# Two bank counts and a filling order in the attention stream of a fused two-layer kernel

## The chip, the cores and the metric

The kernel runs on one core of a Trainium2 chip. The time is the device time of one execution in microseconds: 1094.37 us is the median of three runs of the kernel before (1093.66 to 1094.58). The engines are named as in the profile: PE is the matrix engine (PEld its weight loads), DVE the vector engine, ACT the scalar engine, POOL the general engine, SP the engine that issues most transfers.

## The reference, cut to what matters

The input is x of 2 batches x 512 positions x 512 channels. Four blocks are added to it in turn, each on its layer norm:

```python
x = x + attn_a(_layernorm(x))   # 32 heads of 128, 8 key/value heads, weights as 4-bit codes and scales
x = x + ffn(_layernorm(x))      # 8 low-rank experts (rank 64), the two best of each position, softmax gate
x = x + attn_b(_layernorm(x))   # 32 heads of 16, 8 key/value heads, weights in f32
x = x + ffn(_layernorm(x))      # the same experts again
```

Attention b, which the change is about, is

```python
att = einsum('bhgqd,bhkd->bhgqk', q, k) / sqrt(16)       # q, k turned by the position
att = where(causal, att, -inf)
probs = softmax(att)
out = einsum('bhgqk,bhkd->bhgqd', probs, v) -> (B, T, 512) @ Wo
```

Everything is f32 at the interface.

## The kernel before, in words

The first 60% of the time or so is attention a, and it is not touched by the change. The rest is a sequence with three parts: the first experts ("f1") of both batches with the projections of attention b of batch 0; then the stream, in which the scores of attention b of both batches run while other work fills PE; then an end, with the last output projection and the second experts ("f2") of batch 1.

**The stream.** Attention b has 32 pairs of key heads and query groups (2 batches, 2 halves of the key heads, 4 groups, 2 pairs); each pair takes 3 steps, and all of it 96 steps and 8 more. Two generators are advanced once a step. `maxima` (from L765) multiplies queries with keys into two score banks `sc_b` (L781), and DVE takes each row's maximum out of them (L785); POOL splits the maximum into two parts `mm` (L793, L794); four steps after a pair began, `maxima_in` turns `mm` with PE (`tpm`, L804) and ACT casts it into two rows beside the queries (L807). Eight steps after a pair's maxima, `probabilities` multiplies keys with these longer queries into two banks `st_b` (L828): the scores come transposed and with the maximum taken off. ACT takes the exponential into `pT_b` (L834) and POOL clears what lies above the diagonal (L837). One step's scores are one of three groups: a whole row of 512 columns for two heads, 384 columns, or 128 and 256 together.

Every sixth step `weighted_b` multiplies the probabilities of a group with the values (`num_b`, L854): 32 matmul instructions, in four column strips side by side, into one bank of their own. ACT copies the sums out (L865), and transfers carry the denominators to memory and back for `divided`, which yields the quotients `oN_b` that `output_b` projects (`po`, L910) and adds to x (L914).

**The filling work.** `side` is a chain of generators: the rest of the experts f1 of batch 1 (`py_f`, L266), the projections of batch 1 (normed and turned x `pxT_b`, L178; keys and values `pkv_b`, L674; turned keys `tpk`, L666; queries `pq_b`, L701; turned queries `tpq`, L694), the output projection of batch 0 in two parts, the experts f2 of batch 0 (`pxT_f`, `pg_f` L197, `ph_f` L207, `lg_f` L217, `wT_f` L259, `py_f`), and the first part of the output projection of batch 1. Each `yield` gives the cost of a piece: `MM` = 0.9, about two instructions of 512 columns (one f32 product of 128 rows is two instructions). In each step, after the scores and the value products, pieces are drawn until their costs have used up the `pace` of the step: 0.8 until step 8, 0.95 until step 44, 0.37 until step 66, 0.95 again, 1.4 from step 90.

**Order.** In the stream, `tc.manual_schedule(engines={mybir.EngineType.PE})` keeps PE's instructions in the order of the program; PE runs them in that order, and an instruction that waits holds up all that follow. The other engines' order is planned by the compiler.

**Banks.** PSUM has eight banks. From the end of attention a on they are three pools: `ps_x` with 5 banks for `sc_b`, `st_b` and `tpm` in turn, `ps_n` with 1 for the value products, and `ps_f` with 2 for the filling pieces of the stream (`place("bank", ...)` with `banks = BESIDE`). Outside the stream the experts and projections take their banks from `ps_x` (`ALONE`). A tile of a pool takes the place of the tile that many allocations earlier, and its first matmul waits until the last reader of that one is done. A filling tile is read by `rope_heads` on DVE (L639, L641; for keys also by two copies of the values on ACT, L681), by copies on ACT (L179, L199, L211, L695), by a cast on ACT and a difference on DVE (`halves`, L151, L152), or by a DVE addition or product (L261, L270, L914).

Of the kernel before, what the change touches and what calls it, by code (L numbers as in the profile page):

```python
# [17 lines left out]
PSUM = bass.MemoryType.PSUM  # L18
# [22 lines left out]
def kernel(  # L41
# [113 lines left out]


    MM = 0.9
    def norm_parts(b, which):

        var = small.tile([P, NT, 2], F32, tag="mv", name=f"mv_{which}_{b}")  # L160
        for t in range(NT):
            st = small.tile([P, 6], F32, tag="st", name=f"st_{which}_{b}_{t}")
            nc.vector.bn_stats(st, x[b, t])
            nc.vector.bn_aggr(var[:, t, :], st)
        std = small.tile([P, NT], F32, tag="std", name=f"std_{which}_{b}")
        nc.scalar.activation(std, var[:, :, 1], AF.Sqrt, bias=eps)
        rstd = small.tile([P, NT], F32, tag="rstd", name=f"rstd_{which}_{b}")
        nc.vector.reciprocal(rstd, std)
        yield 3.0
        xT = place("xT", [P, NC, S], f"xnT_{which}_{b}")  # L170
        for t in range(NT):
            xn = place("xn", [P, DM], f"xn_{which}_{b}_{t}")
            nc.vector.tensor_scalar(
                xn, x[b, t], var[:, t, 0:1], rstd[:, t : t + 1], ALU.subtract, ALU.mult
            )
            pt = place("bank", [P, NC, P], f"pxT_{which}_{b}_{t}")
            for c in range(NC):
                nc.tensor.transpose(pt[:, c, :], xn[:, ts(c, P)], ident)  # L178
            nc.scalar.copy(xT[:, :, ts(t, P)], pt)  # L179
            yield MM  # L180
        return xT

    def experts(b, which, store):

        xT = yield from norm_parts(b, which)
        nm = f"{which}_{b}"

        def st(tag, n=1):
            return gate.tile([P, NT, n], F32, tag=tag, name=f"{tag}_{nm}")

        def each(a):
            return a.to_broadcast([P, NT, NE])


        pg = place("bank", [P, S], f"pg_{nm}")
        for c in range(NC):
            nc.tensor.matmul(pg[ts(c, STRIP)], gw[:, c, :], xT[:, c, :], start=True, stop=True)  # L197
        shares = place("xn", [P, S], f"shares_{nm}")
        nc.scalar.copy(shares, pg)  # L199
        yield MM  # L200
        hT = place("hT", [P, NC, S], f"hT_{nm}")

        def ranks(er):

            ph = place("bank", [P, S], f"ph_{nm}_{er}")
            for c in range(NC):
                nc.tensor.matmul(  # L207
                    ph, lora["a"][:, c, ts(er, P)], xT[:, c, :], start=(c == 0), stop=(c == NC - 1)
                )
                if c == NC - 1:  # L210
                    nc.scalar.copy(hT[:, er, :], ph)  # L211
                yield MM

        yield from ranks(0)
        lg = place("bank", [P, NT, NE], f"lg_{nm}")
        for t in range(NT):
            nc.tensor.matmul(lg[:, t, :], shares[:, ts(t, P)], fold, start=True, stop=True)  # L217
        mx, pr, den, rden = st("gmx"), st("gp", NE), st("gden"), st("grden")
        nc.vector.tensor_reduce(mx, lg, AX.X, ALU.max)
        nc.vector.tensor_tensor(pr, lg, each(mx), ALU.subtract)  # L220
        nc.scalar.activation(pr, pr, AF.Exp)
        nc.vector.tensor_reduce(den, pr, AX.X, ALU.add)
        nc.vector.reciprocal(rden, den)
        nc.vector.tensor_tensor(pr, pr, each(rden), ALU.mult)
        yield MM


        best, hot = [], []
        left = pr
        for n in range(2):  # L230
            m, key, km, oh = st(f"m{n}"), st(f"key{n}", NE), st(f"km{n}"), st(f"oh{n}", NE)
            nc.vector.tensor_reduce(m, left, AX.X, ALU.max)
            nc.vector.tensor_tensor(key, left, each(m), ALU.is_equal)
            nc.vector.tensor_tensor(
                key, key, order.unsqueeze(1).to_broadcast([P, NT, NE]), ALU.mult
            )
            nc.vector.tensor_reduce(km, key, AX.X, ALU.max)
            nc.vector.tensor_tensor(oh, key, each(km), ALU.is_equal)
            best.append(m)
            hot.append(oh)  # L240
            if n == 0:
                left = st("left", NE)
                nc.vector.scalar_tensor_tensor(left, oh, -2.0, pr, ALU.mult, ALU.add)
        tot, rtot, w = st("tot"), st("rtot"), st("gw", NE)
        nc.vector.tensor_tensor(tot, best[0], best[1], ALU.add)
        nc.vector.reciprocal(rtot, tot)
        nc.vector.tensor_tensor(w, hot[0], hot[1], ALU.add)
        nc.vector.tensor_tensor(w, w, pr, ALU.mult)
        nc.vector.tensor_tensor(w, w, each(rtot), ALU.mult)
        for er in range(1, NC):  # L250
            yield from ranks(er)
        for t in range(NT):

            we = place("we", [P, NE, RANK], f"we_{nm}_{t}")
            nc.gpsimd.tensor_copy(we, w[:, t, :].unsqueeze(2).to_broadcast([P, NE, RANK]))
            wef = we.rearrange("p e r -> p (e r)")
            tp = place("bank", [P, NC, P], f"wT_{nm}_{t}")
            for er in range(NC):
                nc.tensor.transpose(tp[:, er, :], wef[:, ts(er, P)], ident)  # L259
            part = hT[:, :, ts(t, P)]  # L260
            nc.vector.tensor_tensor(part, part, tp, ALU.mult)  # L261
            yield MM
        for t in range(NT):
            py = place("bank", [P, DM], f"py_{nm}_{t}")
            for c in range(NC):
                nc.tensor.matmul(  # L266
                    py, hT[:, c, ts(t, P)], lora["b"][:, c, :], start=(c == 0), stop=(c == NC - 1)
                )
                if c == NC - 1:
                    nc.vector.tensor_tensor(x[b, t], x[b, t], py, ALU.add)  # L270
                    if store:
                        nc.sync.dma_start(out[b, ts(t, P), :], x[b, t])
                yield MM

# [344 lines left out]
    hlp = ctx.enter_context(tc.tile_pool(name="hl", bufs=1))  # L621
    dram = ctx.enter_context(tc.tile_pool(name="dram", bufs=2, space=bass.MemoryType.DRAM))
    ptp = ctx.enter_context(tc.tile_pool(name="pT2", bufs=6))
    ps_x = ctx.enter_context(tc.tile_pool(name="ps_x", bufs=5, space=PSUM))
    ps_n = ctx.enter_context(tc.tile_pool(name="ps_n", bufs=1, space=PSUM))
    ps_f = ctx.enter_context(tc.tile_pool(name="ps_f", bufs=2, space=PSUM))
    homes.update(xT=(xtp, "xnT"), xn=(temps, "t"), hT=(hp, "hT"), we=(ptp, f"pT{S}"))

    ALONE, BESIDE = [(ps_x, "x")], [(ps_f, "f")]
# [28 lines left out]
    def projections(b):  # L658
# [11 lines left out]
        for t in range(NT):  # L670
            nm = f"b_{b}_{t}"
            pkv = place("bank", [P, DM], f"pkv_{nm}")
            for c in range(NC):
# [1 line left out]
                    pkv[:, :256], xT[:, c, ts(t, P)], wkv2[:, c, :], start=(c == 0), stop=(c == NC - 1)  # L675
                )
                if c == 1:
                    yield MM
            rk = rope_heads(pkv[:, 0:128], B_NKV, t, 0, f"k{nm}")
            for kh in range(2):  # L680
                nc.scalar.copy(  # L681
# [4 lines left out]
                keys_turned(*old)  # L686
            old = t, rk
            yield MM
        qT = qTs[b] = bp.tile([P, NC, S], F32, tag=f"qT{b}", name=f"qT_{b}")

        def queries_turned(t, rq):
# [5 lines left out]
        for t in range(NT):  # L697
            nm = f"b_{b}_{t}"
            pq = place("bank", [P, DM], f"pq_{nm}")
            for c in range(NC):  # L700
                nc.tensor.matmul(  # L701
                    pq, xT[:, c, ts(t, P)], wq2[:, c, :], start=(c == 0), stop=(c == NC - 1)
                )
                if c == 0 and t == 0:
                    keys_turned(*old)
                if c == NC - 1:
                    rq = rope_heads(pq, B_NH, t, 2, f"q{nm}")
                yield MM
            if t:
                queries_turned(*old)  # L710
                yield 0.5
# [191 lines left out]
    def output_b(b, cs):  # L903
# [3 lines left out]
        for i in range(NT):  # L907
            po = place("bank", [P, DM], f"po_{b}_{i}_{cs[0]}")
            for c in cs:
# [2 lines left out]
                )  # L912
                if c == cs[-1]:
                    nc.vector.tensor_tensor(x[b, i], x[b, i], po, ALU.add)  # L914
                yield MM

    def run(*stages):
        stages = list(stages)
# [27 lines left out]
    banks[:], homes["we"] = BESIDE, (wep, "we")  # L946
    side = chain(later, projections(1))
    pace, left = 0.8, 0.0
    for step in range(total + LEAD):
        with tc.manual_schedule(engines={mybir.EngineType.PE}):  # L950
            if step == LEAD:
                pace = 0.95
            if step == half - 4:
                run(side)
                keys_in(1, 0)
                queries_halved(len(pairs) // 2)
                side = output_b(0, (0, 1))
                pace, left = 0.37, 0.0
            if step == half + LEAD:
                keys_in(1, 1)  # L960
            if step == half + LEAD + 10:
                side = chain(side, output_b(0, (2, 3)), experts(0, "f2", True))
                pace, left = 0.95, 0.0
            if step == total - 6:
                side = chain(output_b(1, (0, 1)), side)
                pace, left = 1.4, 0.0
            quotients[:] = [q for q in quotients if next(q, None) is not None]
            p, at = divmod(step + 4, STEPS)
            if at == 0 and p % 4 == 3 and p + 1 < len(pairs) and p + 1 != len(pairs) // 2:
# [5 lines left out]
                maxima_in(p)  # L975
            if LEAD <= step:
                next(ps)
            if step < total:
                next(ms)

            if len(due) > 3 and due[3][0] <= step:
                for _ in range(4):
                    weighted_b(*due.pop(0)[1])
            left += pace
            while left > 0:
                got = next(side, None)
                if got is None:
                    left = 0.0
                else:
                    left -= got  # L990
    banks[:] = ALONE
    while due:
        weighted_b(*due.pop(0)[1])
# [96 lines left out]
```

## Time and profile before

| what | us |
|---|---|
| median of 3 runs (lowest, highest) | 1094.37 (1093.66, 1094.58) |
| the profiled execution's own time | 1095.07 |
| its span | 1093.4 |
| PE busy in the span | 1046.9 |
| DVE, ACT, POOL busy | 859.0, 627.2, 598.5 |
| first maximum's matmul, last value products of the stream's loop | 792.6, 1028.2 |

Busy times are of one profiled execution, on one core. A PE row's end is modelled: rows of PE overlap, and a row can hold a wait of the next one, so distances between starts say more than lengths. In the waits, "A <- B: us, times, longest" gives what an engine's instruction A waited for B. PEld waits overlap the matmul that is still running.

### The profile page before, as it was taken

How to read it: one execution, taken by the hardware profiler on the slowest of the kernel's cores; microseconds unless marked ns; L12 is line 12 of the kernel's file. 1: busy time of each engine (PE TensorE's matmuls, PEld its weight loads, DVE VectorE, ACT ScalarE, POOL GpSimd, SP SyncE). 2: the span in 40 equal slices, each digit the busy share in tenths (PEclk: the TensorE clock that was granted, in tenths of full speed). 3: DMA queues.
4: the chain of work that ended last, by engine and by line, in shares of the span. 5: the costliest groups of instructions: out<-in, count | busy, mean ns of one | idle time of the engine just before them, and what ended most of it. 6: DMA issues, size and time to landing. Idle time of an engine off the chain costs nothing.

```text
span 1093.4 us, 16248 instructions
## 1 busy us (share of the span) xinstructions
PE 1046.9 (96%) x4940; PEld 707.0 (65%) x4940; DVE 859.0 (79%) x2175; ACT 627.2 (57%) x1475; POOL 598.5 (55%) x916
## 2 busy tenths in 40 slices
PE   5799999999999999999999999999999999999988
PEld 3477767777777677777777777556467655565534
DVE  6889899999999999999999999574386667766142
ACT  3666666567666566566666665513166567685410
POOL 2466666677576666666666666262245566554200
PEclk9999999999999999999999999999999999999999
DMA  7301011012110010010021000042342235211011
GB/s 294 116 1 39 1 39 39 1 39 78 39 40 25 16 39 20 20 39 12 28 75 42 1 1 1 1 155 75 87 161 83 57 122 149 88 49 35 28 38 39
DMA packets 23271, 60.47 MB, mean 55 GB/s; under 512 B 4369, under 2 KB 5329, under 8 KB 20369
## 3 DMA queue, kind: packets, MB, share of 16 engines
q1 hardware_dynamic: 23184, 59.44, 16.4%
q8 instruction: 40, 0.66, 0.2%
q14 instruction: 47, 0.38, 0.1%
HBM read 45.53 MB, written 12.85 MB: 53 GB/s over the span
## 4 chain that ended last, share of the span: by engine, by line
PE 80%; DVE 9%; ACT 4%; issue 2%; POOL 2%; DMA 2%; SPq 0%; ACTq 0%; POOLq 0%; DVEq 0%
PE sc L412 11%; PE av L445 11%; PE tp L440 6%; PE ph_f L207 5%; PE ps_q L365 5%; PE ps_o L457 5%; PE ps_o L458 5%; PE ps_q L366 4%; PE st_b L828 4%; PE py_f L266 3%; PE sc_b L781 3%; PE num_b L854 3%; PE po L910 3%; PE pq_b L701 2%; DVE r_q L372 1%
## 5 line engine op out<-in xcount | busy, mean ns | idle before, releaser
L429 POOL TENSOR_SCALAR p<-p,rden 128x128 f32<-128x128 f32 (+3 forms) x256 | 152.4, 607 | 227.0 <-DVE rden L427 167.1
L420 ACT ACTIVATE p<-sc,nmx 128x128 f32<-128x128 f32 (+3 forms) x256 | 135.8, 530 | 110.3 <-DVE nmx L415 108.7
L412 PE MATMUL sc<-kT,qT 128*128 128x128 f32 (+3 forms) x512 | 180.5, 435 | 1.7 <-ACT p L420 1.3
L372 DVE SCALAR_TENSOR_TENSOR r_q<-ps_q,s_q,r_q 128x512 f32<-128x512 f32 x192 | 143.8, 749 | 20.6 <-PE ps_q L366 16.3
L467 DVE SCALAR_TENSOR_TENSOR acc<-ps_o,s_o,acc 128x512 f32<-128x512 f32 x186 | 137.5, 744 | 19.9 <-PE ps_o L458 17.7
L785 DVE CUSTOM_DVE_ANT_0 sc_b<-sc_b,tri 128x128 f32<-128x128 f32 (+3 forms) x256 | 119.8, 517 | 42.2 <-PE sc_b L781 27.8
L445 PE MATMUL av<-pT,v 128*128 128x512 f32 (+3 forms) x512 | 148.5, 433 | 0.0
L445 PEld LDWEIGHTS av<-pT,v 128*128 128x128 f32 x512 | 96.7, 189 | 64.2 <-issue 36.2
L415 DVE CUSTOM_DVE_ANT_0 sc<-sc,tri 128x128 f32<-128x128 f32 (+3 forms) x256 | 125.9, 492 | 11.2 <-PE sc L412 10.3
L441 ACT COPY pT<-tp 128x128 f32<-128x128 f32 (+3 forms) x256 | 108.2, 423 | 46.0 <-PE tp L440 45.6
L365 PE MATMUL ps_q<-xh,w_q 128*128 128x512 f32 x256 | 121.1, 473 | 3.0 <-ACT r_v L370 1.4
L440 PE MATMUL tp<-ident,p 128*128 128x128 f32 x640 | 114.2, 274 | 3.2 <-POOL p L429 1.6
L412 PEld LDWEIGHTS sc<-kT,qT 128*128 128x128 f32 x512 | 94.9, 189 | 27.6 <-ACT p L420 6.9
L457 PE MATMUL ps_o<-ah,w_o 128*128 128x512 f32 x256 | 110.4, 431 | 1.8 <-DVE acc L467 1.2
L366 PE MATMUL ps_q<-xl,w_q 128*128 128x512 f32 x256 | 101.6, 397 | 0.0
L458 PE MATMUL ps_o<-al,w_o 128*128 128x512 f32 x256 | 101.2, 395 | 0.0
L834 ACT ACTIVATE pT_b<-st_b 128x384 f32<-128x384 f32 (+1 forms) x192 | 89.8, 529 | 17.8 <-PE st_b L828 16.7
L440 PEld LDWEIGHTS tp<-ident,p 128*128 128x128 f32 x640 | 78.5, 140 | 31.6 <-issue 8.7
L837 POOL TENSOR_SCALAR_AFFINE_SELECT pT_b<-pT_b 128x128 f32<-128x128 f32 (+1 forms) x192 | 63.4, 339 | 63.6 <-ACT pT_b L834 59.6
L387 POOL TENSOR_TENSOR r_q<-r_q,tab 128x512 f32<-128x512 f32 x64 | 82.2, 1284 | 9.1 <-DVE rs_q L384 9.1
L465 POOL TENSOR_TENSOR acc<-acc,part 128x512 f32<-128x512 f32 x62 | 80.0, 1290 | 11.5 <-ACT part L464 11.5
L388 POOL TENSOR_TENSOR qT<-r_q,rs_q 128x512 f32<-128x512 f32 x64 | 82.6, 1291 | 5.0
(179 smaller groups left out, 2062.9 us busy)
## 6 DMA issues: line engine op xcount, KB each, us to landing
codes_q<-in_q_codes_dram SPq DMA_DIRECT2D x8, 1024.0 KB
codes_o<-in_o_codes_dram SPq DMA_DIRECT2D x8, 1024.0 KB
spread_q<-hl SPq DMA_DIRECT2D x16, 512.0 KB
qs<-spread_q SPq DMA_DIRECT2D x32, 256.0 KB
x_a<-in_x_dram SPq DMA_DIRECT2D x8, 256.0 KB
codes_k<-in_k_codes_dram SPq DMA_DIRECT2D x2, 1024.0 KB
codes_v<-in_v_codes_dram SPq DMA_DIRECT2D x2, 1024.0 KB
x_r<-in_x_dram SPq DMA_DIRECT2D x8, 256.0 KB
```

Source lines behind the costliest of these rows:

```text
L365: nc.tensor.matmul(ps, w[:, c, ts(h, A_HD)], xh[b][:, c, :], start=True, stop=False)
L366: nc.tensor.matmul(ps, w[:, c, ts(h, A_HD)], xl[b][:, c, :], start=False, stop=True)
L372: nc.vector.scalar_tensor_tensor(r, ps, s, r, ALU.mult, ALU.add)
L412: nc.tensor.matmul(sc[:, :n], qT[:, ts(i, P)], kT[:, :n], start=True, stop=True)
L415: nc.vector.tensor_tensor_reduce(sc[:, :n], sc[:, :n], tri[:, S - n :], -(A_HD**-0.5), 3e38, ALU.add, ALU.min, nmx,)
L420: nc.scalar.activation(pr, sc[:, :n], AF.Exp, bias=nmx, scale=-1.0, accum_out=den[:, i % 2 : i % 2 + 1],)
L429: nc.gpsimd.tensor_scalar(prs[j], prs[j], rden[:, j % 2 : j % 2 + 1], 1.0, ALU.mult, ALU.mult)
L440: nc.tensor.transpose(tp[:, j, :], prs[i][:, ts(j, P)], ident)
L445: nc.tensor.matmul(av[:, j * P :], v[:, j, :], pT[:, j, j * P :], start=(j == 0), stop=(j == NT - 1))
L457: nc.tensor.matmul(ps, w[:, h, ts(n, P)], ah, start=True, stop=False)
L458: nc.tensor.matmul(ps, w[:, h, ts(n, P)], al, start=False, stop=True)
L467: nc.vector.scalar_tensor_tensor(to, ps, s, to, ALU.mult, ALU.add)
```

## The change

Four edits to the stream, all in the program's order and its buffers; what is computed stays the same.

1. `ps_x` has 6 banks and `ps_f` 1. With one filling bank, at most one filling tile can be open (begun, and not yet read).
2. So that no second tile is asked for while one is open, the last keys are turned (`keys_turned`) after a further yield and before the first query product, and no longer behind that product's first matmul. A yield in the middle of a tile gives `Open(MM)`; at step `total - 6`, where the output projection of batch 1 is put in front of the chain, an open tile is finished first.
3. A step draws its filling in two halves: half of the pace between the `st_b` matmuls and the `sc_b` matmuls, half at the end of the step.
4. The value products count as `NUM` = 2.1 in the balance of the pace, and each pace from step 8 on is raised by `NUM / 6`.

```diff
+    class Open(float):
+        pass
+
+    def so_far(c, last):
+        return MM if c == last else Open(MM)
...
-                yield MM
+                yield so_far(c, NC - 1)
...
-    ps_x = ctx.enter_context(tc.tile_pool(name="ps_x", bufs=5, space=PSUM))
+    ps_x = ctx.enter_context(tc.tile_pool(name="ps_x", bufs=6, space=PSUM))
     ps_n = ctx.enter_context(tc.tile_pool(name="ps_n", bufs=1, space=PSUM))
-    ps_f = ctx.enter_context(tc.tile_pool(name="ps_f", bufs=2, space=PSUM))
+    ps_f = ctx.enter_context(tc.tile_pool(name="ps_f", bufs=1, space=PSUM))
...
                 if c == 1:
-                    yield MM
+                    yield Open(MM)
...
+        yield MM
+        keys_turned(*old)
...
-                if c == 0 and t == 0:
-                    keys_turned(*old)
...
+    def filled(some):
+        nonlocal left, last
+        left += some
+        while left > 0:
+            last = next(side, None)
+            left = left - last if last is not None else 0.0
+
+    NUM = 2.1
...
             if step == LEAD:
-                pace = 0.95
+                pace = 0.95 + NUM / 6
...
             if step == total - 6:
+                while isinstance(last, Open):
+                    last = next(side)
                 side = chain(output_b(1, (0, 1)), side)
-                pace, left = 1.4, 0.0
+                pace, left = 1.4 + NUM / 6, 0.0
...
             if LEAD <= step:
                 next(ps)
+                filled(pace / 2)
             if step < total:
                 next(ms)
 
             if len(due) > 3 and due[3][0] <= step:
                 for _ in range(4):
                     weighted_b(*due.pop(0)[1])
-            left += pace
-            while left > 0:
-                got = next(side, None)
-                if got is None:
-                    left = 0.0
-                else:
-                    left -= got
+                left -= NUM
+            filled(pace / 2 if LEAD <= step else pace)
```

More of the change, by code (lines that the diff above doesn't have):

```diff
@@ L272, in experts @@
                         nc.sync.dma_start(out[b, ts(t, P), :], x[b, t])
-                yield MM
+                yield so_far(c, NC - 1)
     with ExitStack() as actx:
@@ L677, in projections @@
                 if c == 1:
-                    yield MM
+                    yield Open(MM)
             rk = rope_heads(pkv[:, 0:128], B_NKV, t, 0, f"k{nm}")
@@ L703, in projections @@
                 )
-                if c == 0 and t == 0:
-                    keys_turned(*old)
                 if c == NC - 1:
                     rq = rope_heads(pq, B_NH, t, 2, f"q{nm}")
-                yield MM
+                yield so_far(c, NC - 1)
             if t:
@@ L914, in output_b @@
                     nc.vector.tensor_tensor(x[b, i], x[b, i], po, ALU.add)
-                yield MM
+                yield so_far(c, cs[-1])
     def run(*stages):
@@ L948 @@
     pace, left = 0.8, 0.0
+    last = 0.0
+    def filled(some):
[5 more added lines that the diff above has]
+    NUM = 2.1
     for step in range(total + LEAD):
@@ L957 @@
                 side = output_b(0, (0, 1))
-                pace, left = 0.37, 0.0
+                pace, left = 0.37 + NUM / 6, 0.0
             if step == half + LEAD:
@@ L962 @@
                 side = chain(side, output_b(0, (2, 3)), experts(0, "f2", True))
-                pace, left = 0.95, 0.0
+                pace, left = 0.95 + NUM / 6, 0.0
             if step == total - 6:
+                while isinstance(last, Open):
+                    last = next(side)
                 side = chain(output_b(1, (0, 1)), side)
-                pace, left = 1.4, 0.0
+                pace, left = 1.4 + NUM / 6, 0.0
             quotients[:] = [q for q in quotients if next(q, None) is not None]
```

## The prediction

> **What bounds the kernel now.** I read the page's first two parts, then the stages of the stream, then the waits of TensorE's weight loads in the stream, then the timeline around some filling tiles and at the end.
>
> ```profile
> PE 1046.9 (96%) x4940; PEld 707.0 (65%) x4940; DVE 859.0 (79%) x2175; ACT 627.2 (57%) x1475; POOL 598.5 (55%) x916
> ...
> 800.00:840.00 40.00, 37.45 (x234) 27.21 (x233) 28.68 (x121) 28.20 (x62) 20.54 (x62) 0.96 0.26 83
> 880.00:920.00 40.00, 37.53 (x237) 23.64 (x235) 25.98 (x101) 27.87 (x58) 26.47 (x71) 0.96 0.43 136
> ```
>
> The reader is to see that PE is the busiest engine, and that in the stream (about 792 to 1030 us) DVE and ACT are busy some 70% of a stretch, so neither can be a bound by itself. But a matmul's row has a modelled end and swallows waits, so I rebuilt the stream's PE time from distances between the starts of rows that nothing holds up: 0.43 us for a 512-column filling matmul (16 of them take 6.88 us in the chain), 2.29 for 32 value products, 0.11 for a transpose, 0.46, 0.47 and 0.34 for the three groups of one pair's scores. The stream is 32 pairs x 2 kinds x 1.3 = 83, plus 32 x 0.4 = 13 for turned maxima, 16 x 2.29 = 37 for value products, 143 x 0.43 = 61 for filling, 68 x 0.11 = 7.5 for its transposes and 2 for small ones: 204 us. It lasts 238. Three stretches have a granted clock of 0.96 (4% of 40 us each: 5 us together). So about 29 us are real waits of PE: that is all that smoother scores can give back. The same sum stage by stage gives about 4 until 815, 5 in 815 to 880 (filling dense), 3 in 880 to 894 (no filling), 10 in 894 to 937 (sparse) and 6.5 after it.
>
> ```profile
> PEld st_b L828 <- ACT pT_b L834: 11.0, 37, 0.8
> PEld sc_b L781 <- DVE top L785: 9.8, 26, 1.5
> PEld tpm L804 <- POOL mm L794: 8.1, 10, 1.6
> ...
> PEld st_b L828 <- ACT qs L807: 6.0, 16, 0.8
> ...
> PEld sc_b L781 <- ACT pT_b L834: 3.0, 10, 0.7
> ```
>
> These are waits for a score bank (its last reader is the exponential, the maximum or the cast), except tpm, which waits for data. With five banks in turn and four taken a step, the second bank of a step's st is the one that the first exponential of the step before still reads. A load's wait overlaps the matmul before it, so the 30 us of bank waits here are about 24 on PE.
>
> **The sixth score bank and the new order (gain).** One more bank makes each score wait for a reader half a step older; filling between st and sc gives the exponential 0.86 us more; and after each 2.29 us of value products the stream now goes straight back to scores instead of to another filling piece (before, DVE and ACT stood without work for both). Lower bound of the gain: nothing. Upper: the 24 us of bank waits. I take two thirds, 16.5: 3.5 of the 5 in 815 to 880, 2 in 880 to 894, 5 in 894 to 937 (where DVE and ACT have least slack), 5 after it, 1 before 815.
>
> **One filling bank (cost).** Now every filling tile waits until its predecessor has been read out. How long that takes, counted from the start of the last matmul instruction, is in the timeline:
>
> ```profile
> 828.41 1.02 PE L674 MATMUL pkv_b<-wkv,xnT_b 128*128 128x256 f32 x4
> 829.27 0.27 PE L666 MATMUL tpk<-ident,rot_kb 128*128 128x128 f32 x1
> 830.61 0.33 ACT L681 COPY vpad<-pkv_b 128x64 f32<-128x64 f32 x2
> ...
> 853.44 1.02 PE L701 MATMUL pq_b<-wq,xnT_b 128*128 128x512 f32 x2
> 855.12 0.60 PE L694 MATMUL tpq<-ident,rot_qb 128*128 128x128 f32 x4
> 855.27 0.75 DVE L641 TENSOR_TENSOR rs_qb<-pq_b,tabb 128x256 f32<-128x256 f32 x2
> 855.76 0.59 ACT L695 COPY qT<-tpq 128x512 f32<-128x512 f32 x1
> 896.06 1.02 PE L910 MATMUL po<-wo,oN_b 128*128 128x512 f32 x2
> 897.15 0.68 DVE L914 TENSOR_TENSOR x_r<-x_r,po 128x512 f32<-128x512 f32 x1
> ```
>
> The reader is to see tpk and tpq start in the second bank before pkv and pq have been read: 829.27 against 830.94, and 855.12 against 856.02. Last start to read out: pkv 1.9 us, pq 2.15 (853.87 to 856.02), po 1.33, a copy by ACT 0.9 to 1.2, tpk 1.0. What covers it is the last matmul itself (0.43, a transpose 0.11) and the scores until the next piece: one half-step, about 0.4, a whole step 0.8, plus 0.4 where maxima are turned. Pace 1.3 in two halves puts a 0.9 piece into about seven half-steps of ten. I walked the order of pieces that the yields and paces give, step by step; steps 28 to 32, for one, become: st, last pq1 piece, sc, tpq0 | st, pq2 piece, sc | st, pq2 piece, sc, pq2 piece | st, last pq2 piece, sc | st, tpq1 and first pq3 piece, sc, value products. The switches with a wait:
>
> - pkv straight into tpk, three times, no work between: 1.9 - 0.2 = 1.75 each, 5.3. tpk into pq, nothing between: 1.0. pkv to pkv and tpk to pkv: 0.8 together.
> - pq to its successor, four times, two of them half a step away, two a whole: 1.3, 1.3, 1.0, 1.0, so 4.6. tpq to pq, once with half a step and once with nothing: 1.4. That makes 13.1 for the second projections, against 5 us of waits in that whole stage now.
> - pxT and py of the start: 1.5. po of the first batch: 1.0, two tiles. po of the second, 0.6, 0.2, 0.6, 0.6: 2.0.
> - pxT, pg, ph, lg of the last experts, 0.4 to 0.5 each: 2.2.
> - The last eight steps have no sc any more, so the two halves lie side by side: ph to wT 0.8, four switches of wT 0.6, 1.0, 0.6, 1.0: 4.0.
>
> Sum 23.8 over 33 switches. Everything behind the waiting filling matmul on PE's queue waits too: next st or sc, then the exponential, the maxima, POOL's split and tpm. Some 2 us fall where PE would wait anyway: 22. Lower bound 12 (engines reach the eviction early, and half the switches meet a wait that stays), upper 33 (DVE or ACT first finish two queued score instructions, 0.4 more a switch).
>
> [...]
>
> **The rest.** Value products counted in the pace: the sum of filling per six steps stays 5.7 (6 x 1.3 - 2.1), so no work is added. But the last eight steps have a piece more: the walk ends with two wT and one py tile's first piece (0.45 x 2 + 0.86 = 1.8 us) that the kernel before does after the last value product. There they cost nothing, because the end is set by other things:
>
> ```profile
> 1042.75 1.10 PE L910 MATMUL po<-wo,oN_b 128*128 128x512 f32 x2 [1.28 <-issue]
> ...
> 1052.17 1.88 PE L266 MATMUL py_f<-lora_b,hT_f 128*128 128x512 f32 x4
> 1055.50 2.03 PE L178 MATMUL pxT_f<-ident,xn_f 128*128 128x128 f32 x16 [1.45 <-DVE xn_f L173]
> ```
>
> PE idles 1.28 us before po (the quotients' transfers) and 1.45 after the left-over py pieces at 1052 (the norm). Moved forward, these 1.8 us stand on PE's path and both idles stay or grow: +1.8, bounds 0 and 2.5. Turning the last keys before the queries instead of behind the first product: in the stream it is the 1.0 above; in the first batch other filling lies between: 0, bounds 0 and 1. Marks on open pieces issue nothing. Six banks outside the stream: the waits there are for data, 0, bounds -1 and 0. No DMA, and no step of SP's or POOL's queue, is moved past another.
>
> **Sum.** -16.5 + 22 + 1.8 = +7.3 us on the span of 1093.4: 1100.7. The profiled execution took 1095.07, 1.7 around its span and 0.7 above the median of 1094.37, so the median becomes 1101.7.
>
> **Rivals.**
> - Faster: the freed score banks pay more than the switches cost. Place: 894 to 1010, where filling is sparse and waits are most of the loss. Gain at its bound 24, switches at theirs 12, end 1.8: -10, 1084. It decides from the point where the 33 switches average under 0.45 us (14.7/33). For it: 24 us of bank waits are in the list. Against: 815 to 880 has only 5 us to give, and holds 13 of the cost.
> - The two cancel (switches about 15): 1094.
> - Evictions queue behind scores on DVE and ACT: switches 33 instead of 22: 1113. For it: lg's first read came 1.8 us after its last matmul started (988.51 to 990.33). Against: most others came within 0.3 to 1.0.
> - The sixth bank doesn't do what it says, because the waits are ACT's own pace (a cast pair of 1.16 us, then two exponentials): gain 6, 1112. For it: exponentials follow each other without a gap after each cast (853.90, x4 in 1.92 us).
>
> **How the numbers follow.** Forecast 0.43, faster 0.22, cancel 0.08, late evictions 0.15, bank without effect 0.12. A difference under 0.2% (2.2 us) is what a measurement of this kernel can't tell from none. Slower 0.43 + 0.15 + 0.12 = 0.70, same 0.08, faster 0.22. The forecast's own range is 1097 to 1107 (5 either way, a fifth of the gross terms). Range for 8 in 10: half of the faster case lies over 1088, and the late cases end about 1114: 1088 to 1114.
>
> **What would show it.** In the stream's waits, st and sc on pT and top fall from 24 us (11.0 + 9.8 + 3.0) to under 9; new rows appear where tpk, tpq, pq, pxT, wT or po weight loads wait for vpad, rs_qb, khl, x_r; the stage from the first pkv to the last pq grows by some 8 us and the sparse stage to 937 shrinks by 5; the end from the last value product on keeps its 65 us. I am wrong if the switch waits are short because the scheduler puts evictions first, or if a filling wait gives DVE and ACT just the time that PE lost to them.

## The result, and the profile after

The changed kernel takes 1111.39 us (median of 4 runs, 1108.96 to 1114.3) against 1094.01 before (median of 4). By these medians it is 17.4 us slower, a quotient of 1.0159. The ratio on record is 1.0174, with a 95% interval of 1.0155 to 1.0194; that is 19.0 us, and it implies 1092.4 for the kernel before. The experiments below are compared by such ratios, so their sums are to be held against 19.0 and not against 17.4. The forecast was 7.3 us slower, 1101.7, with a range to 1114. The direction was right and the size was not.

The profiled execution took 1108.96 us, the fastest of the four, with a span of 1107.2. Against the profile before its span is 13.9 us longer. By the start of the turned maxima of a pair, the stages compare so:

| stage | before | after | difference | forecast |
|---|---|---|---|---|
| to the first maxima | 792.6 | 794.0 | +1.3 | 0 |
| pairs 0 to 2 and what precedes them | 22.5 | 27.5 | +5.0 | +0.5 |
| pairs 3 to 11, filling dense | 64.7 | 74.0 | +9.2 | +9.6 |
| pairs 12 and 13, no filling | 14.3 | 12.5 | -1.8 | -2 |
| pairs 14 to 20, filling sparse | 43.6 | 42.3 | -1.3 | -4.7 |
| pair 21 to the loop's last value products | 90.4 | 94.4 | +4.0 | +5.7 |
| from there to the end | 65.2 | 62.6 | -2.6 | 0 |

(The forecast's 2 us of waits that fall together are in no stage.) The +1.3 at the head is not the change's: a kernel below with the same instructions up to there has its first maxima at 792.7. The executions differ in their granted clock, half for 6.8 us from 19.5 in the changed kernel and for 3.4 us from 30.7 in the kernel before. Of the -2.6 at the end, up to 1.7 is a stretch at half clock that only the profile before has there (3.4 us from 1044.5; the fourteen matmuls of po from 1044.36 on take 7.81 us to the next row's start, 0.56 each in place of 0.43).

The stages in between need the same care. A stretch of 3.4 us at half clock takes up to 1.7 us of matrix work with it: the 32 value products at 845.58 in the changed kernel, nearly all inside one, take 3.93 us to the next row's start, and those at 876.62 in the kernel before, at full clock, 2.29. In the stream both executions have 10.2 us of it, but in different stages: the kernel before 3.4 us each from 809.0, 884.1 and 966.0, the changed kernel 6.8 us from 811.4 and 3.4 from 845.5. The windows view of the kernel before shows it stage by stage (stretch, length, busy time of PE, its loads, DVE, ACT and POOL, granted clock, transfers); the one of the changed kernel stands in the last section:

```profile
815.00:880.00 65.00, 64.44 (x425) 42.31 (x424) 43.12 (x171) 41.91 (x94) 38.37 (x107) 1.00 0.26 76
880.00:938.00 58.00, 53.34 (x331) 33.58 (x330) 39.92 (x158) 40.32 (x83) 37.73 (x105) 0.97 0.44 139
938.00:1011.00 73.00, 70.14 (x433) 44.00 (x431) 51.25 (x200) 48.11 (x95) 35.60 (x109) 0.98 0.16 44
```

So up to 1.7 us of the +5.0 and of the +9.2 is the clock's, and without the stretch from 966.0 in the kernel before the +4.0 would be up to 5.7. The -1.8 of pairs 12 and 13 is about what the stretch from 884.1 may be worth alone, so it does not confirm the forecast's -2.

The first view is the list of what PE waited for, in the changed kernel's stream: waiting instruction, what it waited for, us in total, times, longest.

```profile
PE tpm L811 <- POOL mm L801: 8.1, 11, 2.0
PE tpk L673 <- ACT vpad L688: 2.4, 2, 1.3
PE pxT_b L185 <- ACT xnT_b L186: 1.5, 1, 1.5
PE pq_b L710 <- ACT qT L704: 1.4, 2, 0.7
PE po L917 <- DVE x_r L921: 1.3, 3, 0.5
PE tpq L703 <- DVE rs_qb L648: 1.3, 2, 0.7
```

All but the first line are new: a filling tile (tpk, pxT, pq, po, tpq) waits until its predecessor in the one bank has been read out. The timeline of the changed kernel shows one of these waits in full:

```profile
833.45 1.02 PE L681 MATMUL pkv_b<-wkv,xnT_b 128*128 128x256 f32 x4
...
834.58 0.29 DVE L646 TENSOR_TENSOR rc_kb<-pkv_b,tabb 128x128 f32<-128x128 f32 x1 [1.18 <-PE pkv_b L681]
...
835.22 0.52 ACT L688 COPY vpad<-pkv_b 128x64 f32<-128x64 f32 x2 [0.72 <-DVE rs_kb L648]
835.79 0.33 PE L673 MATMUL tpk<-ident,rot_kb 128*128 128x128 f32 x1 [1.32 <-ACT vpad L688]
...
835.88 0.59 PE L788 MATMUL sc_b<-ks,qs 128*128 128x384 f32 x2
...
836.44 0.57 DVE L792 CUSTOM_DVE_ANT_0 sc_b<-sc_b,tri 128x384 f32<-128x384 f32 x1 [1.31 <-ACT khl L151]
```

The reader is to see that tpk starts 0.05 us after the copies of pkv end, that the scores behind it start only then, and that DVE, which would take their maxima, stands idle for 1.31 us meanwhile. The last view, the weight loads' waits in the changed kernel's stream, holds the other half of the story:

```profile
PEld tpm L811 <- POOL mm L801: 11.7, 13, 2.2
PEld sc_b L788 <- issue: 11.4, 44, 1.1
...
PEld sc_b L788 <- DVE top L792: 5.8, 22, 0.8
PEld sc_b L788 <- ACT pT_b L841: 5.3, 19, 0.6
PEld st_b L835 <- DVE top L792: 4.0, 10, 1.1
PEld st_b L835 <- ACT pT_b L841: 3.4, 11, 0.8
```

The waits for a score bank became fewer, but the ones of the turned maxima (tpm) grew from 8.1 to 11.7, and st now waits for DVE where it waited for ACT. (The second line is no loss: a load of 0.19 us behind a filling matmul of 0.43 is not needed earlier.)

For the sums below I counted PE's waits more carefully than in the forecast: an instruction's work begins when its row starts or when its predecessor's spacing has passed, whichever is later, and only time beyond that is a wait. The columns name the PE work that waits; sc, st and tpm are the scores of the maxima, those of the probabilities and the turned maxima. Between the first maxima and the loop's last value products:

| waits of PE, us | filling | sc | st | tpm | value products | sum |
|---|---|---|---|---|---|---|
| before | 5.3 | 13.7 | 8.3 | 6.1 | 1.7 | 35.1 |
| after | 17.8 | 6.9 | 8.9 | 9.8 | 3.7 | 47.2 |

The sums differ by 12.1 us, while that part of the loop is 15.2 us longer (235.5 to 250.7) with the same 10.2 us at half clock. So the count misses some 3 us, and single entries are no better than that.

### The profile page after: what moved, and what is told of

Same layout as the page of the kernel before. It is cut to its first block, busy times and chain, and to the rows that moved or that the text cites. A ratio compares the mean times of both kernels' runs of the same rounds, so it can differ in the third digit from the quotient of the medians.

```text
span 1107.2 us, 16277 instructions
## 1 busy us (share of the span) xinstructions
PE 1047.3 (95%) x4940; PEld 705.0 (64%) x4940; DVE 862.4 (78%) x2175; ACT 626.2 (57%) x1475; POOL 598.4 (54%) x916
## 4 chain that ended last, share of the span: by engine, by line
PE 78%; DVE 11%; ACT 5%; POOL 2%; issue 2%; DMA 2%; SPq 0%; ACTq 0%; POOLq 0%; DVEq 0%
PE sc L419 11%; PE av L452 11%; PE tp L447 6%; PE ps_q L372 5%; PE ps_o L464 5%; PE ps_o L465 5%; PE ps_q L373 5%; PE ph_f L214 4%; PE num_b L861 4%; PE py_f L273 3%; PE st_b L835 3%; PE pq_b L710 2%; PE sc_b L788 2%; PE po L917 2%; DVE r_q L379 1%
## 5 line engine op out<-in xcount | busy, mean ns | idle before, releaser
L474 DVE SCALAR_TENSOR_TENSOR acc<-ps_o,s_o,acc 128x512 f32<-128x512 f32 x186 | 137.4, 744 | 20.1 <-PE ps_o L465 17.8
L472 POOL TENSOR_TENSOR acc<-acc,part 128x512 f32<-128x512 f32 x62 | 79.9, 1289 | 11.5 <-ACT part L471 11.5
```

Source lines behind the costliest of these rows:

```text
L474: nc.vector.scalar_tensor_tensor(to, ps, s, to, ALU.mult, ALU.add)
```

## The experiments

Each time is a median beside runs of the kernel before on the same chip (medians 1092.0 to 1092.6 us), and each ratio is to those, with its 95% interval.

**The banks and the two edits of the order, one by one.** The kernels are the changed one with some of these edits undone. The second edit of the change (the last keys turned earlier, and the marks on open tiles) stays in all of them; it was not undone by itself, so "old order" below still has it, except in the kernel before:

```diff
-    ps_x = ... bufs=6 ...        # five score banks
+    ps_x = ... bufs=5 ...
-    ps_f = ... bufs=1 ...        # two filling banks
+    ps_f = ... bufs=2 ...
-                filled(pace / 2)                                  # no halves
-            filled(pace / 2 if LEAD <= step else pace)
+            filled(pace)
-    NUM = 2.1                                                     # products not counted
+    NUM = 0.0
```

Five and two banks, both edits of the order:

> The changed kernel's order (filling in two halves, value products counted in the pace) with the old banks, five for scores and two for filling. Theory A (the single filling bank is the cost, 12 to 14 us, and the new order moves waits onto the turned maxima): the 33 switch waits are gone, what is left is the order's own few us, 1094 to 1098. Rival B (the order is the cost, the bank counts are not): it stays near the changed kernel, 1105 or more. Rival C (the order is a gain that the single bank hides): under 1091.

Five and one, both edits:

> The changed kernel with one filling bank and only five score banks, so one of the eight banks is unused. Against the changed kernel it prices the sixth score bank alone, against the run with five and two it prices the second filling bank alone. Theory A: the sixth bank is worth about 6 us (the waits of scores for a bank fell from 14.5 to 8.5 us between the two traces), so 1115 to 1119. Rival D (the sixth bank is worth nothing, the waits are DVE's and ACT's own pace): 1110 to 1113. Rival E (it is worth what I forecast, 16 us): 1125 or more.

Six and one, old order:

> Six score banks and one filling bank with the old order: filling at the end of the step alone, value products not counted. Theory A: a filling tile and its successor then have a whole step's scores between them more often, but the switches with nothing between (turned keys behind their product) stay: 1100 to 1106. Rival B (the order is the cost): 1092 to 1098. Rival F (two halves were what kept one bank bearable): over 1113.

Five and two, products counted alone:

> Five score banks, two filling banks, filling at the end of the step as before, but the value products counted in the pace: this edit alone. Theory A: after the value products the scores run without filling and the turned maxima come too early for DVE and POOL, and the work moved before the end costs 1 to 2 us: 1094 to 1098. Rival C (the counted pace is a gain by itself): 1086 to 1091.

Six and one, halves alone:

> Six score banks, one filling bank, filling in two halves, value products not counted. The runs so far: old order with these banks +0.45%, both edits with these banks +1.7%, both edits with the old banks +0.2%. Theory G (the halves set a tile's successor half a step behind it, and one bank makes that a wait; the counted products add little): +1.2% or more, about 1106 to 1111. Rival H (counting the products is what hurts with one bank, since it makes the filling after them denser, 1.3 a step): about +0.5%, 1097 to 1101.

Six and one, products counted alone:

> Six score banks, one filling bank, filling at the end of the step alone, value products counted. Theory G: the cover of a whole step stays for most switches, and counting costs what it cost with the old banks (+0.4%): +0.6 to +1.0%, 1100 to 1104. Rival H: +1.3% or more, 1107 or more.

Five and two, halves alone:

> Five score banks, two filling banks, filling in two halves, value products not counted. With two banks no successor waits, so the halves alone show: since both edits together gave +0.2% and counting alone +0.4%, Theory G expects -0.3 to +0.1%, 1090 to 1095. Rival (the halves cost by themselves, and the two edits make up for each other): +0.4% or more, 1098.

Five and one, old order:

> Old order, five score banks, one filling bank, one of the eight banks unused. It prices the sixth bank and the second filling bank in the old order: with six and one it was +0.45%. Theory A: the sixth bank is worth 2 to 3 us here as in the new order, so +0.65 to 0.75%, 1099 to 1101. Rival E (the sixth bank is worth much more where value products and filling come in one burst): +1.2% or more, 1106. Rival D (nothing): +0.45%.

Measured, as ratio to the kernel before:

| banks (scores, filling) | old order | products counted | halves | both |
|---|---|---|---|---|
| 5, 2 | 1 | 1.0038 [1.0022, 1.0053] | 1.0024 [1.0013, 1.0034] | 1.0017 [1.0006, 1.0028] |
| 5, 1 | 1.0062 [1.0041, 1.0082] | | | 1.0197 [1.0181, 1.0212] |
| 6, 1 | 1.0045 [1.0030, 1.0060] | 1.0065 [1.0043, 1.0087] | 1.0121 [1.0098, 1.0144] | 1.0174 [1.0155, 1.0194] |

What follows: the new order by itself is a small loss (+1.9 us). The second filling bank is worth 19.7 us in the new order (1.0197 less 1.0017) and 6.8 in the old one (with whatever the second edit costs). The sixth score bank is worth 2.5 us in the new order and 1.9 in the old, both taken with one filling bank; each difference is about as wide as its intervals, so rival D, that it is worth nothing, isn't excluded, but 16 is far out of reach of both. It is the halves that make one bank dear (1.0045 to 1.0121): they put a tile's successor half a step behind it. Counted products add to that (to 1.0174), probably because filling then comes at 1.3 a step after each gap. Theory A had the cost in the right place for the new order and priced the sixth bank too high (6 us); for six and one in the old order it missed, 1098.0 for 1100 to 1106, which is inside B's range. B (the order alone is the cost) fell with the run of five and two, and C (the order alone is a gain) with it: most of the loss needs both, one bank and the halves. G held for the halves with one bank; with two banks they cost 0.24%, between what G and its rival expected. H, that with one bank the counting is what hurts, fell, and so did E and F. With two filling banks, counting alone costs 0.38%, more than both edits together.

The waits of the weight loads with five and two banks and the new order show why the order gained nothing:

```profile
PEld sc_b L788 <- DVE top L792: 8.9, 34, 0.8
PEld tpm L811 <- POOL mm L801: 8.4, 10, 1.6
...
PEld st_b L835 <- ACT pT_b L841: 6.2, 22, 0.4
PEld st_b L835 <- DVE top L792: 4.9, 8, 2.3
```

Against the kernel before, st's waits for ACT fell from 11.0 to 6.2 and those for DVE rose from 1.1 to 4.9. The line of the kernel before that this rests on:

```profile
PEld st_b L828 <- DVE top L785: 1.1, 4, 0.5
```

On PE the stream's waits are 33.9 us where they were 35.1: sc 9.3 for 13.7, st 12.6 for 8.3. They changed their place.

**Cover for the filling bank.** The changed kernel, with a half-step without filling behind each piece that closes a tile, and the turned keys of the second batch as pieces of their own:

```diff
+        if closed:
+            closed = False
+            return
         while left > 0:
             last = next(side, None)
             left = left - last if last is not None else 0.0
+            if last is not None and not isinstance(last, Open):
+                closed = True
+                return
...
+            if b:
+                yield MM
             if old:
                 keys_turned(*old)
             old = t, rk
-            yield MM
-        yield MM
+            yield 0.1 if b else MM
+        yield 0.1 if b else MM
         keys_turned(*old)
+        if b:
+            yield 0.1
```

> The changed kernel, but a half-step without filling after each piece that closes a tile, and the second batch's turned keys as pieces of their own (no transposes straight behind the product whose bank they need). The paces and banks are the changed kernel's. Theory G (cover between a tile and its successor is the cost): filling waits in the stream fall from 18 us to 8 or less, 1099 to 1104. Rival I (evictions are simply late on DVE and ACT, whatever stands between): it stays at 1108 or more.

Measured: 1102.07, 1.0095 [1.0070, 1.0121]. Filling waits in the stream fell from 17.8 to 10.7 us. Theory G expected 8 or less there and was right on the time alone; rival I fell. Nearly half of the loss is gone with the same banks and paces, so the distance between a tile and its successor sets that part. What a faster eviction would do was not tried, and 10.7 us of filling waits stay.

**Turned maxima one step later**, in the kernel before and in the changed one:

```diff
-            p, at = divmod(step - 4, STEPS)
+            p, at = divmod(step - 5, STEPS)
             if at == 0 and 0 <= p < len(pairs):
                 maxima_in(p)
```

> The kernel before with one edit: the maxima of a pair are turned one step later (five steps after the pair began in place of four). Theory J (part of PE's waits in the stream is the chain from the last maximum over POOL's split to the turning, 6.1 us in the trace before, which no score bank shortens): these waits fall under 2 us and the time by 2 to 5 us, 1089 to 1092 against 1094. Rival K (they only move to the next wait for a bank): within 1.5 us of the kernel before.

> The changed kernel with the same edit, maxima turned one step later. In its trace the waits for score banks are 8.5 us against 14.5 before, but those of the turned maxima 9.8 against 6.1. Theory J (the sixth bank's gain ran into the turned maxima): the turned maxima's waits fall under 3 us and the time from +1.7% to about +1.1 to 1.3%, 1105 to 1108. Rival K: +1.6 to 1.8%, no change against the changed kernel.

The kernel before didn't change: 1092.81, 1.0005 [0.9993, 1.0016], though its waits of tpm fell from 6.1 to 3.0 us; sc's rose from 13.7 to 16.2. There theory J fell, and K held. The changed kernel went to 1106.05, 1.0119 [1.0096, 1.0143], with tpm's waits at 3.0 in place of 9.8: there J held, at the edge of what it had for the waits.

**Both together in the changed kernel:**

> The changed kernel with a half-step free of filling after each closed tile, turned keys as pieces of their own, and maxima turned one step later. One edit alone took +1.74% to +0.95%, the other to +1.19%. If they add up: +0.4%, 1096 to 1098. If they pay for the same waits: +0.9%, 1101 to 1103.

Measured: 1093.54, 1.0009 [0.9991, 1.0027]. The two edits take back the whole loss, more than either expectation had. Their single effects are -0.79 and -0.55 points, together -1.65; the 0.31 points beyond the sum are about what the intervals of the four runs leave open. The weight loads' waits of this kernel (the stretch goes to 1060, the loop ends at 1026):

```profile
PEld sc_b L792 <- DVE top L796: 7.9, 24, 1.0
...
PEld tpm L815 <- POOL mm L805: 3.8, 2, 3.1
PEld st_b L839 <- DVE top L796: 3.8, 12, 0.6
PEld po L921 <- DVE oN_b L911: 3.6, 3, 1.6
```

The turned maxima's line is down from 11.7 to 3.8 us, and most of the long lines wait for DVE. The filling waits are shorter and not gone: on PE, pkv once and pq twice still wait 1.0 us until DVE has read the tile before. The kernel doesn't beat the kernel before.

**The same cures in the old order** (six and one, filling at the end of a step and ended by a closing piece, turned keys apart, maxima a step later):

> Six score banks and one filling bank, filling at the end of the step alone, value products not counted, a step's filling ends with the piece that closes a tile, the second batch's turned keys are pieces of their own, maxima turned one step later. Every switch of the filling bank then has a whole step's scores as cover. Theories G and J together: filling waits 3 us or less, turned maxima 2 or less, and the sixth bank's 2.5 us stay: 1088 to 1092, faster than both kernels. If the cover isn't what decides, it stays near +0.45%, 1097 to 1099.

Measured: 1093.11, 1.0006 [0.9991, 1.0020]. The loss of +0.45% went, the gain hoped for did not come: filling waits stayed at 7.7 us, sc's at 11.5. The expectation was wrong in that. What went, against six and one in the old order, is the wait of the turned maxima for POOL (in PE's list 6.6 us there, 0.7 here). So the later maxima look like what helped, and the cover did not shorten the filling waits; no run has the two apart in this order.

**What holds the scores.** Four score banks in place of five; maxima over half of each part and not under 20, which leaves out half of that work; one of each pair's two casts on DVE:

```diff
-    ps_x = ... bufs=5 ...
+    ps_x = ... bufs=4 ...
```

```diff
-                        part, part, tri[:, S - n :], 1.0, -3e38, ALU.add, ALU.max,
+                        part[:, n // 2 :], part[:, n // 2 :], tri[:, S - n // 2 :], 1.0, 20.0,
+                        ALU.add, ALU.max,
```

```diff
-            nc.scalar.copy(qs[p % NQ][HALF:HM, h, :].bitcast(F32R), tp[at : at + 2, :])
+            to = qs[p % NQ][HALF:HM, h, :].bitcast(F32R)
+            if h:
+                nc.vector.tensor_copy(to, tp[at : at + 2, :])
+            else:
+                nc.scalar.copy(to, tp[at : at + 2, :])
```

> The kernel before with four score banks in place of five, one of the eight banks unused. Theory L (banks have a steep price that is flat from five on; the sixth was worth 2 to 2.5 us): the fourth to fifth step is worth 8 us or more, 1101 or more. Theory M (the score waits are engines' own pace, banks matter little): 1094 to 1098.

> The kernel before, but DVE takes each maximum over the second half of its scores alone and not under 20, which leaves out half of that part of the computation. DVE's work in the stream falls by some 45 of its 200 us, nothing else changes. Theory M with DVE as the pace: the waits on the maxima (6.5 us for banks, 5 for the turned maxima) go, 1081 to 1085. If the bank count or ACT holds the scores: 1089 or more.

> The kernel before with one of each pair's two casts of the turned maxima moved from ACT to DVE: ACT has 18 us less in the stream, DVE some 20 more. Theory M with ACT as the pace (a cast pair of 1.16 us delays the exponentials that free the banks): 1086 to 1090. If DVE is the pace: 1096 or more. If neither, within 2 us of the kernel before.

Measured: four banks 1111.54, 1.0187 [1.0167, 1.0208]; half maxima 1084.94, 0.9939 [0.9920, 0.9957]; a cast on DVE 1096.75, 1.0042 [1.0026, 1.0059]. So the fifth bank is worth 20 us (with two filling banks) and the sixth 2 to 2.5 (with one): nearly flat from five on, and theory L held. DVE's work is part of what holds the scores: less of it takes 6.7 us off, more of it adds 4.6, although ACT has less to do by the cast. With four banks the loads' waits name the reader that stood in the way:

```profile
PEld sc_b L781 <- ACT qs L807: 18.1, 27, 1.2
...
PEld st_b L828 <- ACT pT_b L834: 10.6, 38, 0.8
PEld st_b L828 <- DVE top L785: 7.7, 16, 1.7
```

The scores of the maxima then wait for the bank of the turned maxima, whose two casts take 1.16 us; with five banks this line was 0.6 us:

```profile
PEld sc_b L781 <- ACT qs L807: 0.6, 1, 0.6
```

No other line of the loads' waits grew as much.

## Why the prediction was right and wrong

**Near in its sum, too high in its switches: the filling bank's cost.** The forecast had 22 us, the runs 19.7 (five score banks, both edits, two filling banks against one). The place was right, but that the sums are so near is luck in part. The 22 was a sum of waits of filling matmuls, 23.8 less what falls together. By the table above these waits rose by 12.5 us (5.3 to 17.8), or some 15 with the 3 that the count misses. The forecast had no term for the rest: other waits behind a held-up queue, and the granted clock. In the two traces that differ in the second filling bank alone, the loop grew from 236.2 to 256.7 us, and its time at half clock from 3.4 to 17.1 (mean granted clock of the two executions 0.997 and 0.989), which is worth up to 6.8.

Some switches came near their rows: pkv into tpk 1.3 and 1.5 (1.75 forecast), tpk into pq 0.95 (1.0), pq into tpq 0.8 twice (1.3), tpq into pq 0.8 twice (0.5 and 0.9), po 0.6, 0.5, 0.6 (0.6). Others hardly waited: the third pkv into tpk 0.1 (1.75), the other two of pq to its successor 0.3 and 0.2 (1.0 each). One was overlooked: the last two tpk follow each other too closely, 1.2 us. The dense stage came out at +9.2 for a forecast of +9.6, and up to 1.7 of it is the half-clock stretch from 845.5.

**Wrong: "I take two thirds, 16.5".** This is the step that failed, the gain of the sixth bank and the new order. The sixth bank gave 2.5 us and the new order -1.9, together 0.6; with the 19.7 of the filling bank that makes the loss 19.1, against 19.0 by the ratio. The step failed in two places.

- The store it drew on, "24 on PE", was too big. I had added up distances between starts that were longer than usual. But a score's row that follows a filling matmul starts early: the one at 853.92 in the profile before starts 0.05 us behind a filling matmul that needs 0.43, and so the distance to the next row is 0.38 too long without any wait. Counted as above, sc and st waited 22.0 us before and 15.8 after; of these, the waits that a reader of a score bank ended were 14.5 before and 8.5 after.
- The 6 us that did go came back at the next thing in the chain: tpm's waits for POOL's split of the maxima rose by 3.7 us on PE, and those of the value products by 2. The pair of runs that differs in the sixth bank alone (five and one, six and one, both edits) shows the same in the loads' waits: sc on top fell from 8.0 to 5.8 and st on pT from 6.7 to 3.4, while tpm on POOL rose from 9.2 (its line stands below) to 11.7. Giving the maxima a step more took 6 us off the changed kernel, but nothing off the kernel before, where the waits moved to sc. What the runs show in place of the 16.5 is a bank curve that is nearly flat from five on and a stream in which DVE's maxima are part of the pace of the scores. The fourth rival, "the sixth bank doesn't do what it says", had this end at 1112, though with a gain of 6, and it put the pace on ACT: moving a cast from ACT to DVE made the time longer, which speaks against that part but adds work to DVE as well.

```profile
PEld tpm L811 <- POOL mm L801: 9.2, 11, 1.6
```

**Wrong: what the waits were to show.** st and sc on pT and top were to fall from 24 us to under 9; they fell from 23.8 to 14.5 on the three lines named (3.4, 5.8, 5.3; sc on pT rose from 3.0), and st on top rose from 1.1 to 4.0.

**The end: +1.8.** The three pieces did not all move. Ahead of the loop's last value products the changed kernel has twelve of the sixteen wT matmuls and the kernel before eight, so one tile moved (0.4 us), and all 32 of py come behind them in both. (With five and two banks all three pieces ran ahead of them.) What did change is that py's last four no longer stand behind po, as they did at 1052.17 before. The timeline of the changed kernel:

```profile
1057.61 1.88 PE L273 MATMUL py_f<-lora_b,hT_f 128*128 128x512 f32 x4
1059.33 7.03 PE L917 MATMUL po<-wo,oN_b 128*128 128x512 f32 x16
1069.21 2.02 PE L185 MATMUL pxT_f<-ident,xn_f 128*128 128x128 f32 x16 [2.85 <-DVE xn_f L180]
```

The idle before pxT grew from 1.45 to 2.85 as forecast, but the one before po, 1.28, is gone. Without the stretch at half clock the end is some 0.9 us shorter, of which the moved tile, now in the loop, is 0.4. So the term came out at about nothing, its lower bound, in place of +1.8.

**The rival that ended on the other side** needed 33 switches under 0.45 us on average. By the runs they cost 19.7 us, 0.6 each, and with a gain of 0.6 us in place of 16.5 they would have had to cost nothing.

**From the profile to the median.** The two profiled executions differ by 13.9 us and the medians by 17.4. The rest goes with the granted clock: the four runs took 1108.96, 1109.27, 1113.51 and 1114.3 us at mean granted clocks of 0.992, 0.992, 0.986 and 0.988. The kernel before has 0.990 to 0.998 in its runs beside the experiments, 0.995 on average, but 0.992 in its profiled execution. That is taken from the runs' clocks and not tested by a run of its own.

## What to carry to other kernels

Price a bank before moving it: the same kernel with one bank left unused shows in one run what the last one is worth (20 us for the fifth here, 2.5 for the sixth), and a list of waits doesn't. If an accumulation bank must be single, look at the work between a tile's last matmul and its successor's first: a half-step left free behind each closed tile, with the turned keys as pieces of their own, took nearly half of the loss away here. And check a sum of waits against spacing over a longer stretch: a wait that is taken away need not pay. In the kernel before, the later maxima took tpm's waits from 6.1 to 3.0 us, sc's rose from 13.7 to 16.2, and the time stayed. Before a stage's difference is read as the change's, see how much of it two executions' clocks explain.

## What the runs showed of the hardware

In the changed kernel's stream the matrix engine's granted clock fell to half twice, for 6.8 us behind a wait of 1.96 us (before tpm at 809.79) and for 3.4 us behind one of 1.02 (before tpk at 843.12). In the windows view of the changed kernel (columns as above), the first two stages of the stream have 0.88 and 0.98:

```profile
792.00:821.00 29.00, 23.50 (x98) 15.87 (x97) 21.61 (x81) 14.59 (x25) 9.75 (x30) 0.88 0.49 159
821.00:895.00 74.00, 65.92 (x412) 41.44 (x411) 42.80 (x173) 40.50 (x90) 38.48 (x105) 0.98 0.21 59
```

The records behind these numbers are one stretch of 6.8 us at half clock from 811.4 and one of 3.4 from 845.5. In the 6.8 us before the second, PE's rows cover 73% and the longest gap is 1.0 us. So gaps of 1.0 to 2.0 us went ahead of a halved clock here. But neither the longest gap nor the covered share tells when it happens: in the same trace the idle of 2.85 us before pxT_f at 1069.21, with PE's rows over 47% of the 6.8 us from 1065.8, was followed by no halved clock (1.00 from 1045 to 1107). What sets it off stays open here. Its price can be bounded: a stretch of 3.4 us at half clock takes up to 1.7 us of matrix work with it, 1.64 in the value products at 845.58. That is more than the wait of 1.02 us ahead of them; whether that wait set the stretch off was not shown.
